# Masked attention with one half in 32 masked on GpSimd, GpSimd in program order, and the last stage's first projections among attention's last sums

## Chip, core and metric

The kernel runs on one core of one Trainium2 chip. The core has five engines that run their own instruction streams side by side: PE (TensorE, matrix products into PSUM), DVE (VectorE), ACT (ScalarE, activation functions), POOL (GpSimd) and SP, which issues DMA transfers. The metric is the device time of one execution in microseconds; lower is better. The kernel before took 3134.0 us (median of three runs, 3131.89 to 3134.24).

## The reference

A graph of 4096 nodes with 256 features passes through two graph attention layers and then one transformer layer whose attention is masked by the same adjacency matrix. The change is in the transformer layer. Cut to what matters:

```python
qkv = layer_norm(x, g1, be1) @ w_qkv            # n = 4096, 8 heads of 32
q, k, v = (qkv[:, 0], qkv[:, 1], qkv[:, 2])
scores = jnp.einsum('nhd,mhd->hnm', q, k) * SCALE
scores = jnp.where((adj != 0)[None, :, :], scores, -jnp.inf)
attn = jax.nn.softmax(scores, axis=-1)
out = jnp.einsum('hnm,mhd->nhd', attn, v).reshape(n, DIM)
x = x + out @ w_proj + b_proj
h2 = layer_norm(x, g2, be2)
return x + jax.nn.gelu(h2 @ w1 + b1) @ w2 + b2
```

## The kernel before

The function `unshifted_transformer` computes the transformer layer in three stages: queries, keys and values; attention; and a last stage with the projection, the second norm and the feed-forward network.

**Attention.** The queries are cut into 8 blocks of 512 (`nb`), the heads into two quads of four (`c`), the keys into 32 tiles of 128 (`mt`). One combination is a unit; there are 512 units, and `units` lists them with `mt` innermost. A unit has two halves `u`, each with two heads. `weights` (line 1863) makes one half: eight score matmuls into a PSUM tile `u_ps` of 128 x 1024 (line 1872; the pool `ps_s` has three such tiles), an exponential on ACT in place (line 1879), and on DVE one `scalar_tensor_tensor` that reads the byte mask from SBUF and the exponentials from PSUM and writes the product to an SBUF tile `u_e` (line 1881; ten such tiles). No maximum is subtracted; a check of the denominators elsewhere decides whether a general version must run.

The masked weights are multiplied with the values (`weigh`, result `u_av`) and summed into denominators (`total`, result `u_dn`). To save matmuls, GpSimd first adds the weights of an odd unit and the one before it (`u_both`, line 2026); units whose `mt // 2 % 8` is 7 are summed without that. Each product or sum is cut into four steps, `PARTS`, each a call of `four` (line 1887) that makes four matmul calls, for the four heads. The matmuls with float32 operands stand twice in the profile, so a step is eight instructions.

**Order.** The loop at line 2010 writes the order of the engines PE, ACT, DVE and SP out by hand (`manual_schedule` with `ordered`, line 2005); GpSimd is not in that set, so its order is the planner's own. Steps wait in the list `waiting` and are taken first in, first out, three behind each half's scores and one more in every eighth half or with a long list (lines 2034 to 2037). A product of unit `i` enters the list at unit `i + 2`, a sum of pairs at `i + 4`. At the end of a quad ACT copies `u_av` and `u_den` out of PSUM (lines 1906 and 1923), and the denominators go through memory to be inverted (`quad_end`, with `later`).

**Last stage.** While the last quad runs, `load_early` (line 1940) loads, paced one step per unit by `pace`, the weights of the last stage and the inputs of its blocks 0 and 1 into SBUF that attention no longer needs: residual rows, attention products `att` and inverted denominators `inv`. Lines 2038 to 2044 then put, for each of the two blocks, two GpSimd operations: residual plus projection bias, and `att` times `inv`. After the loop the last stage begins in a scope of its own, with PE alone in written order and eight PSUM banks in one pool (line 2058). `projected` (line 2071) makes the eight projection matmul calls of a block, adds them to the residual on DVE, and computes the norm's statistics (`norms.moments`: four `bn_stats`, four `bn_aggr`, a square root on ACT) and the normed rows; `turned` (line 2089) transposes them on PE and scales them on ACT. Blocks 0 and 1 are projected first (line 2096), then block 0 is turned (line 2098), and the loop over blocks follows: first feed-forward matmuls (line 2115), GELU on ACT, the next block's projection and turning, second feed-forward matmuls (line 2135).

## Time and profile before

| | |
|---|---|
| median of three runs | 3134.0 us |
| the profiled execution's own time | 3132.63 us |
| its span, first to last instruction | 3130.8 us |
| busy over the whole span | PE 98%, DVE 89%, ACT 86%, POOL 38% |
| attention's first masking waits for its keys until | 1696.5 us |
| last masking on DVE ends | 2862.2 us |
| last copy of the denominators `u_den` on ACT | 2866.0 us |
| first feed-forward matmul | 2875.23 us |
| from there to the end of the span (feed-forward of all eight blocks) | 255.6 us |

In the profile's rows a group is a line, an engine, an operation, its tiles and shapes with the count, then busy time and mean ns of one, then the idle time of the engine just ahead of it and what ended that. In the timeline a row is the start, the duration, the engine, the line and the tiles; instructions of one kind that follow each other are merged, with their count at the end. `PEld` is the loading of matmul weights, which overlaps the matmuls. In a row by stretch, each engine has its busy time and, in brackets, the instructions that it started.

### The profile page before, as it was taken

To read this page: it belongs to the slowest core of one execution; us is meant where nothing else is said; L and a number is where in the kernel's file an instruction comes from. 1 tells how busy PE (TensorE), PEld (TensorE's weight loads), DVE (VectorE), ACT (ScalarE), POOL (GpSimd) and SP (SyncE) were. 2 spreads that over 40 slices of the span, in tenths; PEclk is the share of its full clock that TensorE was granted. 3 is DMA by queue.
4 is the path that set the end of the run, shared out by engine and by line. 5 is a ranking of instruction groups with operands and counts; after the bars stand their busy time and mean duration, and the time that the engine had idled before them with its cause. 6 is when DMAs were issued, how large, how long until landed. Compare 5 with 4: busy or idle time off the path is not lost.

```text
span 3130.8 us, 139193 instructions
## 1 busy us (share of the span) xinstructions
PE 3068.0 (98%) x63976; PEld 2713.3 (87%) x63976; DVE 2777.1 (89%) x3140; ACT 2690.3 (86%) x3340; POOL 1194.4 (38%) x538
## 2 busy tenths in 40 slices
PE   6999999999999999999999999999999999999998
PEld 5899999999889999999975888888888888887766
DVE  7999999999989999999986999999999999997220
ACT  6899999999899999999965999999999999996232
POOL 3300000000330000000002998999998999997110
PEclk8999999999999999999999999999999999999999
DMA  8666555431311313121144101010101100013110
GB/s 261 219 198 207 164 184 156 150 97 30 106 44 31 93 52 97 43 63 43 47 125 142 34 21 38 21 38 28 34 21 34 31 28 28 28 41 105 63 34 22
DMA packets 213170, 250.34 MB, mean 80 GB/s; under 512 B 89120, under 2 KB 133664, under 8 KB 212576
## 3 DMA queue, kind: packets, MB, share of 16 engines
q1 hardware_dynamic: 212576, 241.37, 24.9%
q8 instruction: 502, 8.22, 1.0%
q14 instruction: 92, 0.75, 0.1%
HBM read 198.84 MB, written 42.47 MB: 77 GB/s over the span
## 4 chain that ended last, share of the span: by engine, by line
PE 50%; ACT 1%; DVE 1%; POOL 1%; issue 0%; DMA 0%; SPq 0%; DVEq 0%; ACTq 0%; POOLq 0%
PE u_ps L1872 14%; PE u_av L1890 14%; PE u_dn L1890 8%; PE misc L2135 4%; PE misc L2115 4%; PE bank L1463 3%; PE misc L1810 2%; POOL u_both L2026 1%; PE misc L2076 1%; PE misc L1829 1%; ACT t L1122 1%; PE misc L1556 0%; DVE u_e L1881 0%; DVE t L1137 0%; DVE t L1124 0%
## 5 line engine op out<-in xcount | busy, mean ns | idle before, releaser
L1463 PE MATMUL bank<-vst,t 128*128 128x132 f16 x16384 | 1455.7, 220 | 3.7 <-DVE t L1137 2.9
L2026 POOL TENSOR_TENSOR u_both<-u_e 128x1024 f32<-128x1024 f32 x448 | 1048.0, 2383 | 882.9 <-DMA u_k<-half_d 776.2
L1463 PE MATMUL bank<-vst,mask 128*128 128x132 f16 (+1 forms) x10516 | 1372.2, 206 | 0.0
L1122 ACT ACTIVATE t<-s_b,g_terms 128x1024 int8<-128x1024 f32 x1234 | 1318.6, 1148 | 21.0 <-PE bank L1463 15.2
L1463 PEld LDWEIGHTS <-t 128*128 128x128 fp8e4 x16384 | 1186.1, 96 | 15.6 <-DVE t L1137 5.4
L1881 DVE SCALAR_TENSOR_TENSOR u_e<-u_mask,u_ps 128x1024 f32<-128x1024 uint8 x1024 | 1159.9, 1214 | 9.1 <-DMA u_k<-half_d 4.5
L1879 ACT ACTIVATE u_ps<-u_ps 128x1024 f32<-128x1024 f32 x1024 | 1029.9, 1009 | 117.3 <-PE u_ps L1872 44.1
L1463 PEld LDWEIGHTS <-mask 128*128 128x128 fp8e4 x10516 | 920.4, 98 | 0.0
L1137 DVE SCALAR_TENSOR_TENSOR t<-mask,t 128x2048 int32<-128x2048 int32 x256 | 588.0, 2297 | 74.6 <-ACT t L1122 66.3
L1872 PE MATMUL u_ps<-u_q,u_k 128*32 128x512 f16 x8192 | 637.2, 382 | 6.2 <-DVE u_e L1881 3.8
L1890 PE MATMUL u_av<-u_e,u_v 128*32 128x128 f32 x16384 | 606.3, 273 | 0.0
L1124 DVE TENSOR_SCALAR t<-s_b,g_terms 128x1024 fp8e4<-128x1024 f32 x814 | 590.4, 759 | 2.6 <-DMA s_b<-s_d 2.6
L1890 PEld LDWEIGHTS u_av<-u_e,u_v 128*32 128x32 f32 x16384 | 486.4, 110 | 119.6 <-issue 0.9
L1054 POOL TENSOR_TENSOR vst<-g_adj,vst 128x528 f16<-128x528 f32 x16 | 19.9, 1241 | 725.7 <-ACT g_big L1018 681.6
L1890 PE MATMUL u_dn<-u_both,u_ones 128*32 128x128 f32 x7168 | 282.0, 273 | 2.6 <-POOL u_both L2026 2.5
L1872 PEld LDWEIGHTS <-u_k 128*32 128x32 f16 x8192 | 230.5, 96 | 37.8 <-issue 9.5
L1890 PEld LDWEIGHTS u_dn<-u_both,u_ones 128*32 128x32 f32 x7168 | 215.0, 110 | 54.6 <-POOL u_both L2026 3.7
L2122 ACT ACTIVATE u_hid<-misc,n_b 128x512 f32<-128x512 f32 x64 | 43.9, 687 | 140.2 <-PE misc L2115 140.2
L2135 PE MATMUL misc<-u_k,u_hid 128*128 128x256 f32 x512 | 111.8, 379 | 0.0
L2115 PE MATMUL misc<-ln_cols,u_k 128*128 128x512 f32 x256 | 111.3, 592 | 0.5 <-ACT ln_cols L1559 0.5
L2135 PEld LDWEIGHTS misc<-u_k,u_hid 128*128 128x128 f32 x512 | 96.7, 190 | 13.3 <-issue 0.5
L2115 PEld LDWEIGHTS misc<-ln_cols,u_k 128*128 128x128 f32 x256 | 48.6, 190 | 58.5 <-issue 56.7
(176 smaller groups left out, 1823.1 us busy)
## 6 DMA issues: line engine op xcount, KB each, us to landing
g_adj<-in_adj_dram SPq DMA_DIRECT2D x123, 512.0 KB
s_b<-s_d SPq DMA_DIRECT2D x64, 512.0 KB
mask<-mask SPq DMA_DIRECT2D x128, 256.0 KB
u_mask<-mask SPq DMA_DIRECT2D x64, 256.0 KB
mask<-stage SPq DMA_DIRECT2D x48, 256.0 KB
half_d<-u_halves SPq DMA_DIRECT2D x32, 256.0 KB
u_q<-half_d SPq DMA_DIRECT2D x32, 256.0 KB
rows<-e_x SPq DMA_DIRECT2D x31, 256.0 KB
```

Of the source, the lines that this page charges most:

```text
L1122: nc.scalar.activation(to.bitcast(I8), s, AF.Sign, bias=negd, scale=-1.0)
L1124: nc.vector.tensor_scalar(to, s, negd, -1.0, op0=ALU.is_ge, op1=ALU.mult, saturate=False)
L1137: nc.vector.scalar_tensor_tensor(both, m32.unsqueeze(1).to_broadcast(list(both.shape)), SIGNS, both, op0=ALU.bitwise_or, op1=ALU.bitwise_and,)
L1463: nc.tensor.matmul(to, left, right, start=k not in opened, stop=last)
L1810: nc.tensor.matmul(pq, wq_sb[k][:, i * D + c * P : i * D + (c + 1) * P], hn[:, k, :], start=(k == 0), stop=(k == DC - 1),)
L1872: nc.tensor.matmul(ps[r * O : (r + 1) * O, j, :], k_st[c][:, 2 * u + j, at : at + O], q_st[:, h, :], start=True, stop=True,)
L1879: nc.scalar.activation(ps, ps, AF.Exp, scale=SCALE)
L1881: nc.vector.scalar_tensor_tensor(e, mask, 0.0, ps, op0=ALU.not_equal, op1=ALU.mult)
L1890: nc.tensor.matmul(to[j * O : (j + 1) * O, at], lefts[j], es[j // 2][:, j % 2, at], start=first and part == 0, stop=last and part == PARTS ...
L2026: nc.gpsimd.tensor_tensor(both, es_of[i - 1][u], es_of[i][u], op=ALU.add)
L2115: nc.tensor.matmul(ph, w1_sb[:, k, f * P : (f + 1) * P], hn[:, k, :], start=(k == 0), stop=(k == DC - 1),)
L2135: nc.tensor.matmul(po[:, :D], hid[:, f, at : at + P], w2_sb[:, f, :], start=(f == 0), stop=(f == FC - 1),)
```

## The change

Three things change.

1. In units 0 and 16 of a quad's 32, the first half is masked by GpSimd. Two units ahead, `keep_mask` has ACT turn the byte mask of that key tile into a float32 tile of zeros and ones (`u_one`, by `Sign`). The half's exponential then goes straight to the SBUF tile `u_e`, and GpSimd multiplies it in place with `u_one`, broadcast over the two heads. The very first unit and unit 16 of the last quad are left as they were.
2. GpSimd (`Pool`) joins the engines in written order. The two operations of each block ahead of the last stage (`rows_ready`) change their order among themselves and stand at fixed places: block 0's behind unit 15 of the last quad, block 1's behind the last unit.
3. The projections, norms and the turning of the last stage's first blocks move into attention's scope and stand between its last summing steps, by the table `ending`: `project(0)` behind the last unit's scores, `project(1)` three units later, `turn_first` behind that. They use attention's PSUM tiles. A projection's four residual additions now stand ahead of its statistics on DVE, since DVE's and ACT's order is written there. The last stage's eight banks become two pools of six and two, of which every fourth tile takes the second.

```diff
@@ -1876,10 +1876,24 @@
                         start=True,
                         stop=True,
                     )
-            nc.scalar.activation(ps, ps, AF.Exp, scale=SCALE)
             e = work.tile([P, 2, NB], F32, name="u_e")
-            nc.vector.scalar_tensor_tensor(e, mask, 0.0, ps, op0=ALU.not_equal, op1=ALU.mult)
+            one = kept.pop((nb, c, mt), None) if u == 0 else None
+            if one is None:
+                nc.scalar.activation(ps, ps, AF.Exp, scale=SCALE)
+                nc.vector.scalar_tensor_tensor(e, mask, 0.0, ps, op0=ALU.not_equal, op1=ALU.mult)
+            else:
+                nc.scalar.activation(e, ps, AF.Exp, scale=SCALE)
+                nc.gpsimd.tensor_tensor(
+                    e, e, one.unsqueeze(1).to_broadcast([P, 2, NB]), op=ALU.mult
+                )
             return e
+
+        kept = {}
+
+        def keep_mask(nb, c, mt):
+
+            one = kept[nb, c, mt] = tail.tile([P, NB], F32, name="u_one")
+            nc.scalar.activation(one, block_tiles[nb][1][mt // MC][:, mt % MC, :], AF.Sign)
 
         PARTS = 4
         AFTER = (3, 3, 3, 3)
@@ -1997,6 +2011,24 @@
         both_of = {}
         waiting = []
 
+        def rows_ready(k):
+            res, att, inv = early[k]
+            nc.gpsimd.tensor_tensor(att, att, inv, op=ALU.mult)
+            nc.gpsimd.tensor_tensor(res, res, early["bp"].to_broadcast([P, TB, D]), op=ALU.add)
+
+        last = len(units) - 1
+        ending = {
+            (units.index((NNB - 1, DC - 1, NT // 2 - 1)), 1): [lambda: rows_ready(0)],
+            (last, 1): [
+                lambda: rows_ready(1),
+                lambda: nc.scalar.activation(rooted, norms.eps, AF.Sqrt),
+                lambda: project(0),
+            ],
+            (last + 3, 0): [lambda: project(1)],
+            (last + 3, 1): [lambda: turn_first(0)],
+            (last + 4, 1): [lambda: turn_first(1)],
+        }
+
         def ready(step, i, es):
             waiting.extend(
                 [lambda part=part: step(*units[i], es, part) for part in range(PARTS)]
@@ -2004,8 +2036,41 @@
 
         ordered = {
             mybir.EngineType.PE, mybir.EngineType.Activation, mybir.EngineType.DVE,
-            mybir.EngineType.SP,
+            mybir.EngineType.SP, mybir.EngineType.Pool,
         }
+
+        def project(k):
+            res, att = early[k][:2]
+            pp = ps_s.tile([P, 2, NB], F32, name="u_ps").rearrange("p a (b d) -> p (a b) d", d=D)
+            per = TB // 2
+            for t in range(TB):
+                for c in range(DC):
+                    nc.tensor.matmul(
+                        pp[:, t, :],
+                        att[:, c, t * P : (t + 1) * P],
+                        early["wp"][:, c, :],
+                        start=(t % per == 0 and c == 0),
+                        stop=(t % per == per - 1 and c == DC - 1),
+                    )
+            for t in range(TB):
+                nc.vector.tensor_tensor(res[:, t, :], res[:, t, :], pp[:, t, :], op=ALU.add)
+            both = norms.moments(res)
+            if k == 0:
+                two = blocks.tile([P, 2, TB * D], F32, name="u_q")
+                res_n = two[:, 0].rearrange("p (t d) -> p t d", t=TB)
+                early["hn"] = two[:, 1].rearrange("p (c n) -> p c n", c=DC)
+            else:
+                res_n = masks.tile([P, TB, D], F32, name="u_mask")
+            norms.normed(res_n, res, both)
+            nc.gpsimd.tensor_tensor(
+                res, res, early["b2"].to_broadcast([P, TB, D]), op=ALU.add
+            )
+            early[k] = res, res_n
+
+        def turn_first(c):
+            norms.turned(
+                early["hn"], c, early[0][1], ps_a.tile([P, NB], F32, name="u_av"), 2
+            )
         scope.enter_context(tc.manual_schedule(engines=ordered))
         for i in range(len(units) + 5):
             for u in range(HC // 2):
@@ -2021,6 +2086,10 @@
                     if u == 0:
                         pace()
                     es_of.setdefault(i, []).append(weights(*units[i], u))
+                    if u == 0 and i + 2 < len(units) and units[i + 2][2] % 16 == 0 and (
+                        units[i + 2] != (NNB - 1, DC - 1, NT // 2)
+                    ):
+                        keep_mask(*units[i + 2])
                     if i % 2 == 1 and not alone(mt):
                         both = work.tile([P, 2, NB], F32, name="u_both", bufs=6)
                         nc.gpsimd.tensor_tensor(both, es_of[i - 1][u], es_of[i][u], op=ALU.add)
@@ -2035,15 +2104,8 @@
                 count = AFTER[i % 2 * 2 + u] + more
                 for _ in range(min(count, len(waiting))):
                     waiting.pop(0)()
-            for k, unit in enumerate(((NNB - 1, DC - 1, NT // 2 - 1), units[-1])):
-                if i < len(units) and units[i] == unit:
-                    res, att, inv = early[k]
-                    nc.gpsimd.tensor_tensor(
-                        res, res, early["bp"].to_broadcast([P, TB, D]), op=ALU.add
-                    )
-                    nc.gpsimd.tensor_tensor(att, att, inv, op=ALU.mult)
-            if i == len(units) - 1:
-                nc.scalar.activation(rooted, norms.eps, AF.Sqrt)
+                for step in ending.get((i, u), ()):
+                    step()
             if i % 2 == 0 and later:
                 later.pop(0)()
         assert not waiting and not pacing
@@ -2055,7 +2117,16 @@
         big = scope.enter_context(tc.tile_pool(name="u_big", bufs=1))
         ln = scope.enter_context(tc.tile_pool(name="u_ln2", bufs=2))
         tail = scope.enter_context(tc.tile_pool(name="u_ff", bufs=2))
-        ps_m = scope.enter_context(tc.tile_pool(name="u_ps_m", bufs=8, space=PSUM))
+        banks = [
+            scope.enter_context(tc.tile_pool(name=f"u_ps_m{k}", bufs=n, space=PSUM))
+            for k, n in enumerate((6, 2))
+        ]
+        used = []
+
+        def bank():
+            used.append(None)
+            return banks[len(used) % 4 == 0].tile([P, NB], F32, name="misc")
+
         wp_sb, w1_sb, w2_sb = early["wp"], early["w1"], early["w2"]
         bp_sb, b2_sb = (early[name].to_broadcast([P, TB, D]) for name in ("bp", "b2"))
 
@@ -2071,7 +2142,7 @@
         def projected(res, att):
 
             for t in range(TB):
-                pp = ps_m.tile([P, NB], F32, name="misc")
+                pp = bank()
                 for k in range(DC):
                     nc.tensor.matmul(
                         pp[:, :D],
@@ -2089,13 +2160,13 @@
         def turned(res_n):
             hn = ln.tile([P, DC, NB], F32, name="ln_cols")
             for c in range(DC):
-                norms.turned(hn, c, res_n, ps_m.tile([P, NB], F32, name="misc"), 2)
+                norms.turned(hn, c, res_n, bank(), 2)
             return hn
 
         scope.enter_context(tc.manual_schedule(engines={mybir.EngineType.PE}))
-        ready = [projected(*early[nb][:2]) for nb in range(2)]
+        ready = [early[nb] for nb in range(2)]
         coming = rows_of(2)
-        hn = turned(ready[0][1])
+        hn = early["hn"]
 
         def check_dens():
             inside = big.tile(list(dens.shape), F32, name="u_inside")
@@ -2110,7 +2181,7 @@
             more = nb + 1 < NNB
             hid = tail.tile([P, FC, NB], F32, name="u_hid")
             for f in range(FC):
-                ph = ps_m.tile([P, NB], F32, name="misc")
+                ph = bank()
                 for k in range(DC):
                     nc.tensor.matmul(
                         ph,
@@ -2130,7 +2201,7 @@
                 hn = turned(ready[0][1])
             for t in range(TB):
                 at = t * P
-                po = ps_m.tile([P, NB], F32, name="misc")
+                po = bank()
                 for f in range(FC):
                     nc.tensor.matmul(
                         po[:, :D],
```

## The prediction

> **What bounds the kernel now.** I read the page's busy shares and slices first (attention runs from 1696 to 2866 us), then its costliest groups, the busy time by stretch, and last single instructions of the timeline. Four groups carry attention:

> ```profile
> L2026 POOL TENSOR_TENSOR u_both<-u_e 128x1024 f32<-128x1024 f32 x448 | 1048.0, 2383 | 882.9 <-DMA u_k<-half_d 776.2
> L1881 DVE SCALAR_TENSOR_TENSOR u_e<-u_mask,u_ps 128x1024 f32<-128x1024 uint8 x1024 | 1159.9, 1214 | 9.1 <-DMA u_k<-half_d 4.5
> L1879 ACT ACTIVATE u_ps<-u_ps 128x1024 f32<-128x1024 f32 x1024 | 1029.9, 1009 | 117.3 <-PE u_ps L1872 44.1
> ```

> 1024 halves (512 units, two head pairs each) pass through PE, ACT and DVE. VectorE's masking is busy for 1159.9 us of an 1166 us stage: it sets the pace. A stretch from the middle agrees:

> ```profile
> core 0: us, PE busy (x) PEld busy (x) DVE busy (x) ACT busy (x) POOL busy (x), PEclk, DMA share, GB/s
> 2300.00:2400.00 100.00, 100.00 (x2920) 81.76 (x2916) 100.00 (x90) 90.38 (x102) 89.27 (x40) 1.00 0.11 33
> ```

> PE also reads 100%, but its ends are modelled, so I take its own pace from the starts of score groups. In the PE timeline before a boundary of two head quads:

> ```profile
> 2418.54 0.61 PE L1872 MATMUL u_ps<-u_q,u_k 128*32 128x512 f16 x8
> ...
> 2419.84 0.62 PE L1872 MATMUL u_ps<-u_q,u_k 128*32 128x512 f16 x8
> ...
> 2420.93 0.62 PE L1872 MATMUL u_ps<-u_q,u_k 128*32 128x512 f16 x8
> ...
> 2424.20 0.61 PE L1872 MATMUL u_ps<-u_q,u_k 128*32 128x512 f16 x8
> ...
> 2425.33 0.61 PE L1872 MATMUL u_ps<-u_q,u_k 128*32 128x512 f16 x8
> ```

> A half with four summing steps behind its scores takes 1.30 us (2418.54 to 2419.84), one with three 1.09 us (three halves from 2420.93 to 2424.20). The last gap, 1.13 us, waits: a score needs the PSUM tile of three halves earlier, which VectorE gives back. Order by line 2034 is one four-step half in eight: 7 x 1.09 + 1.30 = 8.93 us for eight. VectorE takes 1.133 us per half (31 in 35.19 us below, (35.19 - 1.21)/30), 9.06 for eight. So PE is only 0.13 us per eight halves, 1.5%, behind VectorE: relieving VectorE soon meets PE.

> **How much earlier VectorE can start.** These are the timeline's exponential and maskings around unit 0 of a quad; I match them by counting halves back from the copy of `u_num`, which follows unit 2's first exponential:

> ```profile
> 2422.68 1.01 ACT L1879 ACTIVATE u_ps<-u_ps 128x1024 f32<-128x1024 f32 x1
> 2422.93 2.35 DVE L1881 SCALAR_TENSOR_TENSOR u_e<-u_mask,u_ps 128x1024 f32<-128x1024 uint8 x2
> ```

> The second masking of that pair starts at 2424.06 (1.133 after 2422.93) and reads what ACT finished at 2423.69. The first is the half that GpSimd would mask. Take it away, and the next can start at 2423.69 plus some 0.03 us: 0.34 us earlier, not 1.13. ACT's lead, not VectorE's freed time, is what one removal can win. Afterwards VectorE runs without gaps again, and PE must catch up those 0.34 us at 0.13 per eight halves, about 21 halves of the 32 until the next removal, so each removal meets the same state.

> Two ACT copies eat into that lead in a quad's first units:

> ```profile
> 2425.99 1.01 ACT L1879 ACTIVATE u_ps<-u_ps 128x1024 f32<-128x1024 f32 x1
> 2426.91 0.59 ACT L1906 COPY u_num<-u_av 128x512 f32<-128x512 f32 x1
> 2427.39 1.95 ACT L1879 ACTIVATE u_ps<-u_ps 128x1024 f32<-128x1024 f32 x2
> ```

> The exponential behind the copy ends at 2428.42, and its masking starts at 2428.58: lead 0.16. With VectorE 0.34 earlier and PE 0.05 to 0.09 ahead by then, it stalls some 0.14; the `u_den` copy two halves later costs about 0.08 more. Of 0.34, 0.12 is left.

> [...] For the new Sign on 128x512 [...] the trace's copies of that size took 588 and 596 ns[...]. [...] Here Sign (line 1122) and Exp (1018, 1019) alternate in the graph layers with no load at those lines[...]. [...] The masking has one SBUF and one PSUM input; it took 1.21 to 1.22 us both beside a busy and beside an idle GpSimd (idle 2423.1 to 2426.49), so no contention shows. [...]

> **Part 1, the masks.** The condition picks units 0 and 16 of each quad's 32, first pair only: 32 halves, less the very first (no unit two ahead of it) and the excluded last: 30. Each removes one masking (1.133 us of VectorE), adds one Sign on ACT, and one multiply on GpSimd.
> Sign: an extra copy of that size delayed the next exponential by about 0.29 us beyond ACT's usual gap (lead 0.45 to 0.16). It stands behind half 28 of 32, where the lead is 0.45: no stall. Behind it on ACT are the exponentials, and VectorE waits for those. Uncovered it would cost 0.29 x 30 = 9 us.
> Multiply: no row has exactly this form; line 2044's multiply took 2.38 to 2.40 us and line 2041's add with a broadcast operand 2.35 to 2.39, so 2.35 at the issue pace; bounds 2.3 and, say, twice. GpSimd does 14 sums and then rests:

> ```profile
> 2426.49 32.78 POOL L2026 TENSOR_TENSOR u_both<-u_e 128x1024 f32<-128x1024 f32 x14 [3.38 <-DVE u_e L1881]
> ```

> The multiply falls into that 3.4 us rest, and `weigh` of the unit comes 6 to 7 halves later in the written order (steps of unit 16 are popped in units 19). Hidden; GpSimd's 16-unit total becomes 15 x 2.34 = 35.1 of about 36.2.
> Gain: 15 removals at unit 16 x 0.34 = 5.1; 15 at unit 0 x 0.12 = 1.8. Sum 6.9 us.

> **Part 2, program order on GpSimd.** Before, its four operations for the last stage were issued early, among the last quad's sums:

> ```profile
> 2803.15 2.39 POOL L2041 TENSOR_TENSOR u_k<-u_k 128x1024 f32<-128x1024 f32 x1
> ...
> 2821.83 2.35 POOL L2041 TENSOR_TENSOR u_q<-u_q,u_k 128x1024 f32<-128x1024 f32 x1
> ...
> 2828.81 2.38 POOL L2044 TENSOR_TENSOR u_q<-u_q,u_mask 128x1024 f32<-128x1024 f32 x1
> 2831.16 32.76 POOL L2026 TENSOR_TENSOR u_both<-u_e 128x1024 f32<-128x1024 f32 x14
> ```

> and VectorE, the bound, lost time exactly there:

> ```profile
> 2821.89 1.22 DVE L1881 SCALAR_TENSOR_TENSOR u_e<-u_mask,u_ps 128x1024 f32<-128x1024 uint8 x1 [1.05 <-POOL u_both L2026]
> 2825.34 1.22 DVE L1881 SCALAR_TENSOR_TENSOR u_e<-u_mask,u_ps 128x1024 f32<-128x1024 uint8 x1 [2.23 <-ACT u_ps L1879]
> 2827.03 35.19 DVE L1881 SCALAR_TENSOR_TENSOR u_e<-u_mask,u_ps 128x1024 f32<-128x1024 uint8 x31 [0.47 <-ACT u_ps L1879]
> ```

> 1.05 + 2.23 + 0.47 = 3.75 us. In written order only two operations (4.7 us) stand behind unit 15, in the 3.4 us rest (unit 16's multiply is left out there). GpSimd is then some 1.3 us late, growing by 0.16 per pair of units (two sums, 4.69, against four halves, 4.53) to 2.3 us; the sums' matmuls come about 7.4 us after a pair's first sum can start and need 4.7, so up to 2.7 us late is covered. Gain 3.75; without that cover, 0.

> **Part 3, the tail.** Before: last masking ends 2862.2, sums end 2866.0, 32 projection matmuls of block 0 and 1 from 2866.64 (7.17 us), turning 0.87, first feed-forward matmul 2875.23, and since that stage took 14.00 instead of 13.73, its effective start is 2875.5. The change moves the same PE work (3.45 x 2 + 0.87) between the 28 summing steps of 0.22 us: PE from 2859.5 has 6.1 + 7.8 us, to 2873.4. But ACT now runs in written order: block 1's square root stands ahead of block 0's turning. Projection 1 ends about 2870.3 (GpSimd's product for it is ready near 2865.9), four adds, four statistics (0.42 each) and four aggregates follow to 2872.9; root to 2873.25, turning 0 to 2874.0; the second turning needs the same PSUM tile, then `u_den`'s copy, and ends 2875.4. Start again 2875.4: gain 0.1, taken as nothing. Bounds: 1.5 gained if root 1 is early; 1.5 lost if the denominators' copy, now 8 us later, delays the queued `inv_d` loads for block 2 on SP (projection 2 is due 13.8 us after the start). The new bank order reuses each of eight banks after eight tiles, as before: nothing.

> **Sum.** 6.9 + 3.75 + 0 = 10.65 us. Against the profiled execution, 3132.63 (span 3130.8 and 1.8 around it), 3122.0. The median shown is 1.4 above that execution: 3134.0 - 10.65 = 3123.4.

> **Rivals.**
> B, PE's floor is reached: if ACT's lead grows after a removal, each of 30 periods gains 32/8 x 0.13 = 0.53, 16 us, plus 3.75: 3114. For it: PE has that slack. Against: ACT's lead in the lines above.
> D, little comes through: Sign or the copies eat the masks' gain, or GpSimd is late in the last quad anyway. 3.75 or 6.9 alone: 3127 to 3130.
> C, slower: GpSimd becomes the bound. A 16-unit period has 36.26 us (32 x 1.133) against 14 x 2.34 = 32.8 plus the multiply; it decides from 3.5 us. At twice the price, 4.7 us, the period is 37.5: +1.2 x 30 = 37, less 3.75: 3167. Against: both nearest rows cost 2.4.

> **Chances.** Mine 0.55 (3119 to 3127.5), B 0.18 (3109 to 3119), D 0.17, C 0.10. A measurement tells 0.2%, 6.3 us, from no change, so D mostly counts as same: faster 0.72, same 0.18, slower 0.10. The range reaches from B's lower part to D's end, 3110 to 3132; my own case alone is 3119 to 3127.5.

> **What would show it.** Right: 994 maskings at line 1881's successor, VectorE idle of about 0.8 us at each kept half put down to ACT, a period of 32 halves of about 36.0 us where it was 36.26, no wait for GpSimd's sums near unit 20 of the last quad, first feed-forward matmul about 13 us after the last masking. Wrong: a Sign with table loads, a multiply above 3.5 us, PE waits for `u_both` in every period, or periods of 35.7 us (B).

## The result and the profile after

The changed kernel took 3124.36 us (median of eight runs, 3120.02 to 3125.99) against 3132.43 us for the kernel before (eight runs on the same chips): a ratio of 0.9973, 95% interval 0.9964 to 0.9982, so 8 us or 0.27% faster. The forecast was 3123.4 and a gain of 10.65. The profiled execution took 3124.94 us with a span of 3123.2, 7.7 and 7.6 us less than before.

I split the span at two events. *Attention* is the time from the start of the first masking on VectorE to the end of the last. The *tail* is the time from there to the effective start of the feed-forward stage: block 2's first projection matmul less the 13.73 us that an undisturbed feed-forward stage takes ahead of it. The forecast's own count put that start at 13.3 before and 13.2 after.

| | first masking | attention | tail | time of the profiled execution |
|---|---|---|---|---|
| before | 1696.50 | 1165.72 | 13.12 | 3132.63 |
| after | 1696.62 | 1155.67 | 15.17 | 3124.94 |
| forecast for after | as before | 1155.1 | 13.2 | 3122.0 |

So attention gave 10.05 us and the tail took 2.05 back; the first masking comes 0.12 later, and from block 2's projection to the end the span has 0.2 us more.

The rows of the costliest groups after the change (line 1883 is the former 1881, 1882 the former 1879, 2095 the former 2026):

```profile
L2095 POOL TENSOR_TENSOR u_both<-u_e 128x1024 f32<-128x1024 f32 x448 | 1047.9, 2388 | 805.1 <-DMA u_k<-half_d 775.6
L1883 DVE SCALAR_TENSOR_TENSOR u_e<-u_mask,u_ps 128x1024 f32<-128x1024 uint8 x994 | 1131.5, 1213 | 26.8 <-ACT u_ps L1882 25.8
L1882 ACT ACTIVATE u_ps<-u_ps 128x1024 f32<-128x1024 f32 x994 | 996.4, 1008 | 93.0 <-PE u_ps L1872 33.6
```

30 maskings have left VectorE, but its idle time has grown from 9.1 to 26.8 us, nearly all put down to ACT. One masking costs what it did (1213 against 1214 ns). The added work, from the list of all groups:

```profile
L1886 POOL TENSOR_TENSOR u_e<-u_e,u_one 128x1024 f32<-128x1024 f32 x30 | 71.6, 2387 | 0.5
L1885 ACT ACTIVATE u_e<-u_ps 128x1024 f32<-128x1024 f32 x30 | 30.9, 1030 | 4.2
L1896 ACT ACTIVATE u_one<-u_mask 128x512 f32<-128x512 uint8 x30 | 18.7, 624 | 0.2
```

The multiply takes 2.39 us, Sign 0.62 with no table load at its line (the 19 loads at other lines took 1.28 us each), and the exponential that writes to SBUF 1.03 against 1.01 us. VectorE's timeline shows where its idle time lies: once at each of the 30 kept halves.

```profile
1734.44 35.22 DVE L1883 SCALAR_TENSOR_TENSOR u_e<-u_mask,u_ps 128x1024 f32<-128x1024 uint8 x31 [0.71 <-ACT u_ps L1882]
1770.34 15.13 DVE L1883 SCALAR_TENSOR_TENSOR u_e<-u_mask,u_ps 128x1024 f32<-128x1024 uint8 x13 [0.69 <-ACT u_ps L1882]
```

The gap in the row is counted from the end of the last masking, which overlaps the next by 0.08 us; 1.133 - 0.08 - 0.71 = 0.34 us is what the removal wins at once, the number that was worked out from ACT's lead. In the last quad GpSimd now runs as written, and VectorE's last row has no gap where there were three:

```profile
2815.80 2.40 POOL L2016 TENSOR_TENSOR u_k<-u_k 128x1024 f32<-128x1024 f32 x1
2818.13 2.42 POOL L2017 TENSOR_TENSOR u_k<-u_k 128x1024 f32<-128x1024 f32 x1
2820.46 32.75 POOL L2095 TENSOR_TENSOR u_both<-u_e 128x1024 f32<-128x1024 f32 x14
```

```profile
2795.71 56.58 DVE L1883 SCALAR_TENSOR_TENSOR u_e<-u_mask,u_ps 128x1024 f32<-128x1024 uint8 x50
```

The tail is the part that went worse. ACT's timeline, and then PE's:

```profile
2864.24 0.30 ACT L1526 ACTIVATE n_mean<-n_mean,n_eps 128x4 f32<-128x4 f32 x1 [6.35 <-DVE n_mean L1521]
2864.45 0.76 ACT L1559 ACTIVATE u_q<-u_av,n_be,n_g 128x512 f32<-128x512 f32 x1
```

```profile
2865.26 0.82 PE L1556 MATMUL u_av<-ident,u_q 128*128 128x128 f32 x4 [1.99 <-ACT u_q L1559]
2865.88 15.47 PE L2186 MATMUL misc<-u_q,u_k 128*128 128x512 f32 x32
```

Block 0's first turning was ready on PE at 2862.5, but on ACT it stands behind block 1's root (2864.24), which waits for VectorE's statistics; the second turning needs the same PSUM tile, so PE rests 1.99 us. Then the feed-forward stage takes 15.47 instead of 14.00 us. The busy time by stretch names the reason, in the column `PEclk`, the clock that PE was granted (1.00 is full):

```profile
core 0: us, PE busy (x) PEld busy (x) DVE busy (x) ACT busy (x) POOL busy (x), PEclk, DMA share, GB/s
2862.00:2865.90 3.90, 1.91 (x33) 1.48 (x33) 3.50 (x15) 1.44 (x3) 0.00 (x0) 0.96 0.23 59
2865.90:2869.20 3.30, 3.30 (x6) 1.31 (x6) 0.28 (x1) 0.78 (x1) 2.88 (x2) 0.53 0.97 330
2869.20:2875.00 5.80, 5.80 (x15) 2.63 (x14) 2.69 (x6) 3.65 (x5) 1.76 (x1) 1.00 0.51 131
```

From 2865.9 to 2869.2 PE was granted 0.53 of the clock and made only six matmuls; the clock record of the trace has the half clock from 2865.62 to 2869.03, right behind the rest.

### The profile page after: what moved, and what is told of

It is laid out like the page before. It is cut to its first block, busy times and chain, and to the rows that moved or that the text cites. A ratio compares the mean times of both kernels' runs of the same rounds, so it can differ in the third digit from the quotient of the medians.

```text
span 3123.2 us, 139201 instructions
## 1 busy us (share of the span) xinstructions
PE 3061.6 (98%) x63976; PEld 2713.3 (87%) x63976; DVE 2747.7 (88%) x3110; ACT 2699.7 (86%) x3370; POOL 1265.1 (41%) x568
## 4 chain that ended last, share of the span: by engine, by line
PE 51%; ACT 1%; DVE 1%; issue 0%; DMA 0%; DVEq 0%; ACTq 0%
PE u_ps L1872 15%; PE u_av L1904 14%; PE u_dn L1904 8%; PE misc L2186 4%; PE misc L2206 4%; PE bank L1463 3%; PE misc L1810 2%; PE misc L1829 1%; ACT t L1122 1%; PE misc L2147 1%; PE misc L1556 0%; DVE t L1137 0%; DVE t L1124 0%; DVE u_e L1883 0%; PE u_ps L2048 0%
## 5 line engine op out<-in xcount | busy, mean ns | idle before, releaser
L1122 ACT ACTIVATE t<-s_b,g_terms 128x1024 int8<-128x1024 f32 x1234 | 1318.7, 1148 | 21.0 <-PE bank L1463 15.2
L1883 DVE SCALAR_TENSOR_TENSOR u_e<-u_mask,u_ps 128x1024 f32<-128x1024 uint8 x994 | 1131.5, 1213 | 26.8 <-ACT u_ps L1882 25.8
L1882 ACT ACTIVATE u_ps<-u_ps 128x1024 f32<-128x1024 f32 x994 | 996.4, 1008 | 93.0 <-PE u_ps L1872 33.6
L1872 PE MATMUL u_ps<-u_q,u_k 128*32 128x512 f16 x8192 | 632.4, 381 | 7.0 <-DVE u_e L1883 4.5
L1872 PEld LDWEIGHTS <-u_k 128*32 128x32 f16 x8192 | 229.5, 96 | 29.2 <-issue 8.9
L2206 PEld LDWEIGHTS misc<-u_k,u_hid 128*128 128x128 f32 x512 | 96.7, 190 | 13.3 <-issue 0.5
L2186 PE MATMUL misc<-ln_cols,u_k 128*128 128x512 f32 x224 | 97.3, 592 | 0.0
L867 DVE TENSOR_SCALAR adj<-g_adj 128x1024 fp8e4<-128x1024 int32 x123 | 88.9, 723 | 3.8 <-DMA g_adj<-in_adj_dram 3.8
```

The lines of the kernel that those rows point to most:

```text
L867: nc.vector.tensor_scalar(v.rearrange("p m r -> p r m"), loaded.pop((nb, c, i)), 1.0, -(2.0**-30), op0=ALU.min, op1=ALU.max, saturate=False,)
L1122: nc.scalar.activation(to.bitcast(I8), s, AF.Sign, bias=negd, scale=-1.0)
L1872: nc.tensor.matmul(ps[r * O : (r + 1) * O, j, :], k_st[c][:, 2 * u + j, at : at + O], q_st[:, h, :], start=True, stop=True,)
L1882: nc.scalar.activation(ps, ps, AF.Exp, scale=SCALE)
L1883: nc.vector.scalar_tensor_tensor(e, mask, 0.0, ps, op0=ALU.not_equal, op1=ALU.mult)
L2186: nc.tensor.matmul(ph, w1_sb[:, k, f * P : (f + 1) * P], hn[:, k, :], start=(k == 0), stop=(k == DC - 1),)
```

## The experiments

The theory after the result: (1) one removed masking wins ACT's lead at that place, not VectorE's freed time; (2) written order on GpSimd won the stall in the last quad; (3) the tail lost 2 us because ACT's written order puts block 1's root ahead of block 0's turning. The rivals are in the expectations. Each is judged by the two stretches of its trace; times are of whole runs.

| kernel | attention | tail | time |
|---|---|---|---|
| `e1_no_masks` | 1161.69 | 13.74 | 3129.07 |
| `e2_old_tail` | 1155.33 | 12.30 | 3120.50 |
| `e3_root_behind` | 1155.98 | 11.84 | 3120.79 |
| `e4_four_at_0` | 1158.54 | 15.19 | 3127.59 |
| `e5_unmasked` | 1156.54 | 13.75 | 3124.61, one run |
| `e6_twice` | 1202.41 | 14.24 | 3170.76, one run |
| `e7_four_at_4` | 1155.10 | 15.28 | 3125.98, one run |
| `e8_unit16` | 1157.66 | 13.75 | 3127.24, one run |
| `e9_late_and_4` | 1155.20 | 11.97 | 3120.21 |
| `e10_changed_again` | 1154.79 | 13.74 | 3123.70 |

Attention's length varies by up to a microsecond between executions of one kernel, mostly in its first 10 us: the changed kernel took 1155.67 in one and 1154.79 in another. The first had the half clock from 1698.26 to 1701.68 and a wait of VectorE of 0.72 us behind it; the second had neither. Where less than that matters I use the time of a quad, averaged over 14 of them from VectorE's starts: 72.54 us without masks, 72.15 with them.

**Without GpSimd's masks.**

```diff
-                    if u == 0 and i + 2 < len(units) and units[i + 2][2] % 16 == 0 and (
-                        units[i + 2] != (NNB - 1, DC - 1, NT // 2)
-                    ):
-                        keep_mask(*units[i + 2])
```

> All of the change except GpSimd's masks: VectorE masks every half again. Theory that the parts add up (written order on GpSimd removes the 3.75 us stall in the last quad, the masks are worth about 0.39 us per quad): the last masking ends near 2858.4 us of the span, 3.75 earlier than before the change and about 6 later than with it; no idle time of VectorE put down to ACT in the steady part; time about 6 us above the changed kernel. Rival, the masks gave the whole 9.9 us and the order nothing: last masking near 2862. Rival, the order gave nearly all of it: last masking at 2853 to 2854.

Attention took 1161.69 us: 4.03 less than before the change, 6.02 more than with it. So the written order gave 4.0 and the masks 6.0 us, and both rivals fall. The medians of the two kernels, from different chips, lie 4.7 us apart, and by the ratios to before, 0.9991 and 0.9973, it is 5.6; their intervals are too wide to tell either from 6. The tail in the profiled execution is 13.74 us: it has the same 1.98 us rest of PE, but the clock stayed full behind it. The ratio to before is 0.9991 (0.9983 to 1.0): the change without its masks is hardly a gain, since the tail takes back a part of what the order gives (0.6 of 4.0 in this trace).

**The tail as it was.**

```diff
-                lambda: project(0),
             ],
-            (last + 3, 0): [lambda: project(1)],
-            (last + 3, 1): [lambda: turn_first(0)],
-            (last + 4, 1): [lambda: turn_first(1)],
...
-        ready = [early[nb] for nb in range(2)]
+        ready = [projected(*early[nb][:2]) for nb in range(2)]
         coming = rows_of(2)
-        hn = early["hn"]
+        hn = turned(ready[0][1])
```

> The change without its third part: masks and written order on GpSimd stay, but the projections, norms and turning of blocks 0 and 1 stand behind attention again, as before the change. Theory that the moved tail costs 2 us: last masking ends where it does with the change (2852.3), the first feed-forward stage starts in effect 13.1 us later as before the change (2865.4 where the changed kernel has 2867.5), no stretch of half clock near 2866; time about 2 us below the changed kernel. Rival, the tail loss is noise or comes from the earlier end of attention: start again near 2867.5.

The tail fell to 12.30 us and the time to 3120.5, 0.9964 of before (0.9952 to 0.9977): the change is better without its third part. The interval overlaps the changed kernel's, so this rests on the tail in the trace as much as on the medians. Attention keeps its length, so the third part has no share in the gain there. 12.30 is also less than the 13.12 of before and than the 13.1 expected: PE waited 0.61 us for GpSimd's last sums there, and does not here.

**Block 1's norm behind block 0's turning.**

```diff
-            (last + 3, 0): [lambda: project(1)],
+            (last + 3, 0): [lambda: project(1, whole=False)],
             (last + 3, 1): [lambda: turn_first(0)],
-            (last + 4, 1): [lambda: turn_first(1)],
+            (last + 4, 1): [lambda: turn_first(1), lambda: norm(1)],
...
-        def project(k):
+        products = {}
+
+        def project(k, whole=True):
...
-            pp = ps_s.tile([P, 2, NB], F32, name="u_ps").rearrange("p a (b d) -> p (a b) d", d=D)
+            pp = products[k] = ps_s.tile([P, 2, NB], F32, name="u_ps").rearrange("p a (b d) -> p (a b) d", d=D)
...
+            if whole:
+                norm(k)
+
+        def norm(k):
+            res, pp = early[k][0], products[k]
             for t in range(TB):
                 nc.vector.tensor_tensor(res[:, t, :], res[:, t, :], pp[:, t, :], op=ALU.add)
```

> The changed kernel, but block 1's residual additions, statistics, root and norm are written behind block 0's two turnings; its projection matmuls stay where they are. Theory (block 0's turning waits in ACT's queue behind block 1's root, PE then rests 2 us, and the granted clock halves for 3.4 us): no wait of PE before the second turning, no half clock there, first feed-forward stage starting in effect near 2864.5 instead of 2867.5, time about 3 us below the changed kernel. Rival, the projections' work on PE and VectorE sets the start: within 1 us of 2867.5.

ACT's timeline of this kernel now has the turning first and the root behind the second one:

```profile
2861.88 0.78 ACT L1559 ACTIVATE u_q<-u_av,n_be,n_g 128x512 f32<-128x512 f32 x1 [4.63 <-PE u_av L1556]
...
2863.41 0.78 ACT L1559 ACTIVATE u_q<-u_av,n_be,n_g 128x512 f32<-128x512 f32 x1
2864.09 0.29 ACT L1526 ACTIVATE n_mean<-n_mean,n_eps 128x4 f32<-128x4 f32 x1
```

and PE's second turning no longer waits:

```profile
2861.77 0.86 PE L1904 MATMUL u_dn<-u_e,u_ones 128*32 128x128 f32 x24
2862.71 0.66 PE L1556 MATMUL u_av<-ident,u_q 128*128 128x128 f32 x4
```

The tail is 11.84 us, 3.3 less than in the changed kernel, and the second turning took 0.66 us on PE instead of 0.82; the time is 3120.79, 0.9964 of before (0.9951 to 0.9976). The rival falls. Against the old tail the moved projections are worth 0.5 us, which the times cannot tell apart.

**The four-step half moved: ACT's lead made smaller, and larger.** The number in the condition of line 2034 (2103 after the change) is changed to 0 in one kernel and to 4 in another.

```diff
-                more = (2 * i + u) % 8 == 6 and len(waiting) > 3 or len(waiting) > 5 * PARTS
+                more = (2 * i + u) % 8 == 0 and len(waiting) > 3 or len(waiting) > 5 * PARTS
```

> The changed kernel with the four-step half moved by two halves, so that it is the half whose mask GpSimd makes: the next half's scores come later. Theory that ACT's lead sets what one removal wins: the lead at that half falls from 0.37 to 0.28 us, VectorE's idle time at each of the 30 kept halves grows from 0.70 to about 0.79 us, time 1 to 3 us above the changed kernel. Rival, the win is what VectorE frees until PE's own pace stops it: idle times and time unchanged.

> The changed kernel with the four-step half moved two halves earlier than it was, to halves 28 and 4 around the kept half 0. Theory of ACT's lead: the lead at half 1 is 0.45 instead of 0.37, so VectorE's idle time at a kept half falls from 0.70 to about 0.62; the four-step half at 4 then costs about 0.08 of it again, so first to last masking stays at 1154 to 1156.5. Rival, PE's pace: idle time stays at 0.70 or grows.

VectorE's timeline of the first and then of the second:

```profile
1735.11 35.26 DVE L1883 SCALAR_TENSOR_TENSOR u_e<-u_mask,u_ps 128x1024 f32<-128x1024 uint8 x31 [0.80 <-ACT u_ps L1882]
```

```profile
1735.80 35.27 DVE L1883 SCALAR_TENSOR_TENSOR u_e<-u_mask,u_ps 128x1024 f32<-128x1024 uint8 x31 [0.63 <-ACT u_ps L1882]
```

The gap went from 0.71 to 0.80 and to 0.63 us, as ACT's lead at that place went from 0.37 to 0.28 and to 0.45. (The leads are those of the kernel before: 0.28 us for the half right behind a four-step one, 0.37 for the third behind it, 0.45 for the fifth.) With 0 attention is 2.9 us longer (30 x 0.09 = 2.7), a quad takes 72.37 us, and the median is 3.2 us longer. With 4 a quad takes 72.11, so only 0.04 of the 0.16 that two larger leads would give stays. VectorE's starts, half by half against those of the kernel before, show where the rest goes: each kept half wins 0.42 us at once; behind unit 16 0.33 of it lasts (0.29 in the changed kernel), behind unit 0 0.09, no more than in the changed kernel. That the four-step half at half 4 takes it, as was expected, is not shown. VectorE frees the same time and PE does the same work in all three kernels; only the lead differs, and what a removal wins at once follows it.

**Are Sign and the multiply hidden?** One kernel leaves both out, the other makes the multiply twice.

```diff
-                nc.gpsimd.tensor_tensor(
-                    e, e, one.unsqueeze(1).to_broadcast([P, 2, NB]), op=ALU.mult
-                )
...
-            one = kept[nb, c, mt] = tail.tile([P, NB], F32, name="u_one")
-            nc.scalar.activation(one, block_tiles[nb][1][mt // MC][:, mt % MC, :], AF.Sign)
+            kept[nb, c, mt] = True
```

> The changed kernel with ACT's Sign and GpSimd's multiply left out: the 30 kept halves go on unmasked, so their weights are not the reference's. From the first to the last masking the changed kernel takes 1155.7 us, without any GpSimd masks 1161.7. Theory that both added operations are hidden (Sign in ACT's lead, the multiply in GpSimd's rest): 1155.7 within 0.5, VectorE's idle time at the kept halves still 0.70. Rival, Sign costs what one more copy on ACT would if it stalled VectorE, up to 0.29 x 30 = 9 us, or GpSimd is what PE waits for: 1147 to 1154.

A quad takes 72.21 us without the two, 72.15 with them: they cost nothing. (Attention's 1156.54 is outside the 0.5 that was stated, to the long side, which no cost of theirs explains. The 0.06 per quad that make it up are lost at the first masking behind the copy of `u_num`, 0.17 us there instead of 0.11; why is open.)

```diff
-                nc.gpsimd.tensor_tensor(
-                    e, e, one.unsqueeze(1).to_broadcast([P, 2, NB]), op=ALU.mult
-                )
+                for _ in range(2):
+                    nc.gpsimd.tensor_tensor(
+                        e, e, one.unsqueeze(1).to_broadcast([P, 2, NB]), op=ALU.mult
+                    )
```

> The changed kernel with GpSimd's multiply made twice in a row (zeros and ones, so the second changes nothing). Theory that GpSimd is covered only up to some 3.5 us: its 16-unit total becomes 14 x 2.34 + 2 x 2.35 = 37.5 us against the period of 36.07, so it sets the pace: a quad takes 75 instead of 72.15 us, first to last masking 1194 to 1200 us, time near 3166. Rival, the sums are not on the path (the matmuls wait long enough in their list): 1156 to 1160.

GpSimd's timeline, without a rest:

```profile
2002.72 32.82 POOL L2096 TENSOR_TENSOR u_both<-u_e 128x1024 f32<-128x1024 f32 x14
2035.45 4.88 POOL L1887 TENSOR_TENSOR u_e<-u_e,u_one 128x1024 f32<-128x1024 f32 x2
2040.41 32.80 POOL L2096 TENSOR_TENSOR u_both<-u_e 128x1024 f32<-128x1024 f32 x14
```

Its 16 units take 37.69 us (2002.72 to 2040.41) and set the pace: attention is 46.7 us longer, the time 3170.8. That is a little more than expected, 1202.4 against 1194 to 1200, as two multiplies with the 14 sums cost 0.2 us more than reckoned. The cover is real and short: one multiply leaves GpSimd some 1 us of rest per 16 units.

**Unit 16 only.**

```diff
-                    if u == 0 and i + 2 < len(units) and units[i + 2][2] % 16 == 0 and (
+                    if u == 0 and i + 2 < len(units) and units[i + 2][2] == 16 and (
```

> The changed kernel with GpSimd masking unit 16 only, 15 halves instead of 30. Theory: a removal at unit 16 wins 0.34 us, one at unit 0 only 0.05 to 0.12, since the copies of u_num and u_den eat the lead there: first to last masking 1156.3 to 1157.5, against 1155.7 with both and 1161.7 with none. Rival, both win the same 0.20: 1158.7.

A quad takes 72.29 us: 0.25 less than without masks, 0.14 more than with both; attention is 0.16 us above its range. The order is as expected, a removal at unit 16 being worth more than one at unit 0. Two of the 14 quads took 72.62, each with a further gap of VectorE of 0.28 to 0.29 us just behind the kept half, which the profile puts down to nothing in one and to GpSimd's multiply in the other. The other twelve took 72.24, so a removal at unit 16 wins 0.30. The changed kernel's own trace gives the split without these gaps: half by half against the kernel before, VectorE is 0.34 us ahead right behind either kept half, and of that 0.29 lasts behind unit 16 and 0.09 behind unit 0.

**Both helpful edits, and the changed kernel again beside it.** The first is the edit of block 1's norm with the four-step half at 4.

> The two helpful edits together: block 1's norm behind block 0's turning, and the four-step half at 28 and 4. Theory: the first takes 3 us off the tail (first feed-forward stage in effect 11.8 us behind the last masking instead of 15.2), the second 0.04 us off each quad; time 3 to 4 us below the changed kernel, near 3120.5, and PE never waits for block 0's turning. Rival, the tail's gain was a chance of the clock: within 1 us of the changed kernel.

> The changed kernel itself, as the measure for the one beside it on the same chip: 3124.4 within 1.5 us. Its tail again has PE's wait of 2 us before the second turning; whether the clock halves behind it may differ from the first profile, where it did: the first feed-forward stage starts in effect 13.7 us behind the last masking with the full clock, 15.2 with the half one.

On one chip: 3120.21 us (3118.72 to 3120.69) against 3123.70 (3119.63 to 3124.80) for the changed kernel and 3131.77 before, ratios 0.9962 (0.9948 to 0.9976) and 0.9972 (0.9961 to 0.9983). The intervals overlap; that the first is better by some 3 us rests on the traces (tail 11.97 against 13.74 or 15.17) as much as on the medians. The profiled execution of the changed kernel had the full clock this time (1.00 in every stretch from 2855 to 2875), and the tail of 13.74 us named for it.

## Why the prediction was right, by its steps

The time forecast, 3123.4, is within a microsecond of the 3124.36 measured, and that is in part luck: the gain was forecast at 10.65 us and is 8.07, and the median that it was taken from, 3134.0 of three runs, lay 1.57 above the 3132.43 of eight. Of the terms the masks were 0.9 too large, the order 0.3 too small, and the tail lost 2.05 where nothing was put.

**ACT's lead as the limit: right.** The step that decided between this forecast and case B was that a removed masking of 1.133 us wins only 0.34. The gap of 0.71 at every kept half says the same, and the two kernels with the lead changed moved it by about the change of the lead. Case B, PE's floor, would have needed periods of 35.7 us; they were 36.07.

**The masks' sum: right in kind, a little too large.** 6.9 us forecast, 6.0 measured (0.39 per quad instead of 0.46). Both terms were a little high: unit 16 keeps 0.29 us of 0.34, since the next three maskings stall by 0.05 in all; unit 0 keeps 0.09 where 0.12 was worked out. There VectorE loses 0.11 and 0.09 us at the two maskings behind the copies of `u_num` and `u_den`, where the prediction had 0.14 and 0.08, so the path that it named is the one in the trace. (The mean of the second copy is 598 ns, not 596; nothing hangs on it.)

**Sign and the multiply at nothing: right.** Both covers exist: leaving the two out won nothing. The cover of the multiply ends between 2.4 us, which cost nothing, and 4.9; that it ends near 3.5, as was worked out, was not tested closer. At twice the price GpSimd sets the pace, and case C came out at 3171 where 3167 was worked out. The neighbouring rows, 2.38 and 2.39 us, were the right price.

**GpSimd in written order: right.** 3.75 forecast, 4.0 measured with the masks taken out. The three gaps were not waits alone: the busy time by stretch of the kernel before shows PE at a reduced clock (0.61 from 2823 to 2826) behind its wait for GpSimd, which ended at 2821.91.

```profile
2820.00:2823.00 3.00, 1.11 (x24) 0.98 (x26) 1.95 (x2) 0.62 (x2) 3.00 (x2) 0.82 0.32 107
2823.00:2826.00 3.00, 3.00 (x58) 2.41 (x53) 0.77 (x2) 1.02 (x2) 3.00 (x2) 0.61 0.07 21
```

The sum of the gaps held both, so it was right without its parts being known.

**The tail at nothing, within 1.5 us: mis-sized.** It lost 2.05. The order on ACT, root 1 ahead of turning 0 ahead of the second turning, was named and is what happened, and moving the norm away removed the loss. But the working had projection 1 end 8.1 us and the root begin 10.7 us after the last masking; they were 8.8 and 11.95. Not all of that is lost, since the feed-forward stage begins (2865.88) before ACT has scaled the second turning (2866.12), for which the working let it wait. With the full clock the tail is 13.74 us, 0.6 more than before. The other 1.4 us are the halved clock, which the working did not have at all; of two profiled executions of the changed kernel one had it and one had not, with tails of 15.17 and 13.74 us. The bound of a later load for block 2 didn't come into play: its product on VectorE was made at 2873.3, 8 us ahead of its projection.

## What to carry to other kernels

Taking one masking of 1.133 us out of VectorE, the engine that sets the pace here, won at once only the 0.34 us that ACT's lead at that place allowed; read such a lead off the timeline (supplier's end to consumer's start) and count the removals, before counting freed busy time. When an engine joins a written order, look at what stands ahead of each instruction on it: here one root of 0.3 us, with the statistics that it waits for, written ahead of two turnings, cost in the profiled execution as much as a third of the masks' gain (2.05 of 6.0 us), and writing it behind the work that was ready won it back (tail 11.84 instead of 15.17 us). GpSimd, with a rest of 3.4 us per 16 units, took one operation of 2.4 us for nothing (a quad in 72.15 us with it, 72.21 without) and not two (attention 46.7 us longer).

## What the runs showed of the hardware

The granted clock fell to 0.50 for 3.41 us behind rests of PE of only 2 us: in the kernel before behind 1.89 us in which it waited for GpSimd (half clock from 2821.94 to 2825.36), and in the tail of the changed kernel behind 1.99 us in which it waited for ACT (2865.62 to 2869.03).

| execution | rest of PE | clock behind it |
|---|---|---|
| kernel before, wait for GpSimd | 1.49 to 3.38 | half |
| changed kernel | 1.07 to 3.05 | half |
| `e7_four_at_4` | 1.11 to 3.09 | half |
| `e4_four_at_0` | 1.40 to 3.38 | half |
| `e10_changed_again` | 1.80 to 3.78 | full |
| `e5_unmasked` | 1.97 to 3.95 | full |
| `e6_twice` | 2.36 to 4.35 | full |
| `e8_unit16` | 3.00 to 4.98 | full |
| `e1_no_masks` | 3.25 to 5.24 | full |

In the traces of the kernel before and the changed kernel, their first 30 and last 15 us left out, five steps at the full clock had rests of PE of 1.99 us or more in sum, and the half clock followed each; it also followed one with 1.84, but not one with 1.94, and none with 1.65 or less. The rests ahead of attention show the same of equal lengths: in the kernel before PE rested 2.42 us from 1689.80, 2.33 of them in one step, and had the half clock from 1692.13; in the changed kernel it rested 2.43 us from 1690.56, 0.88 in one step and 1.55 in the next, and kept the full clock until 1698.26, behind a further rest of 3.43 us. This is read from the traces; no run moved a rest on purpose. If a rest of 1.98 us is as likely to begin anywhere, it falls inside one step in (3.41 - 1.98) / 3.41 = 0.42 of cases, an estimate from these figures; here it was three of eight. In the two profiled executions of the changed kernel the rest of 2 us came with a tail of 15.17 us in one and 13.74 in the other, and it fits that the changed kernel's runs, 3119.6 to 3126.0, spread wider than those of the two kernels without the rest, 3118.7 to 3121.2.
